# Three PSUM banks for the convolutions, transposes two heads behind, rank tables behind the sixth block

## The chip, the cores and the metric

The kernel runs on one core of a Trainium2 chip. The metric is the device time of one execution in microseconds (us); where several executions were timed, their median. The core's engines run beside each other and meet at semaphores: TensorE (PE: matmuls, with a separate row PEld for its weight loads), VectorE (DVE), ScalarE (ACT), GpSimd (POOL) and the queues that issue DMAs (SPq, ACTq, POOLq). The profile's times count from the first instruction of the profiled execution.

## The reference

`x` is 128 rows (batch) of 32 heads of 512 positions. A state-space layer turns each head into a causal convolution with a kernel computed from the parameters, and masks each row at its own length. The 4096 resulting tokens of 512 values go through a mixture of 16 experts (four per token) plus one shared expert, and the sum is added to `x`:

```python
K = _get_kernel(log_dt, C, log_A_real, A_imag, L)      # 32 heads x 512
y = irfft(rfft(u, 2 * L) * rfft(K, 2 * L))[..., :L] + u * D[:, None]
y = y * (arange(L) < length[:, None])                  # (128, 32, 512)
scores = sigmoid(y @ gate_w.T) + bias                  # 16 experts
topk_w, topk_idx = top_k(scores, 4)                    # normalised to weights cw
out = sum over e of (silu(y @ Wg[e].T) * (y @ Wu[e].T) * cw[e]) @ Wd[e].T
out = x + out + silu(y @ Sg.T) * (y @ Su.T) @ Sd.T
```

## The kernel before

The work has three stages. From 0 to about 125 us it builds the convolution kernels and convolves the 32 heads; from there to about 268 us it runs the shared expert over all tokens (eight units, `unit_step`) while it sorts the tokens by expert (`slots`); after that it runs the experts over sorted tiles of 128 tokens (`turn_of`). The change lies in the first stage.

**Heads and blocks.** Four heads make a block `tb` (eight blocks). The loop near the end of the first stage takes heads 0 and 1 alone and then pairs (2,3), (4,5) to (30,31). For a pair, `convolve` (L601) runs four matmuls a head on TensorE into a PSUM bank `py` (L607), and VectorE multiplies the bank by the length mask into `yb` (L625). I call this product "mask h". Behind each head `behind_head` (L951) issues other work: on given heads the next piece of the convolution kernels (`waves`, on VectorE and ScalarE, and `kernels`, on VectorE and GpSimd with small matmuls into `pk`, L407, read by `krow`, L415), the load of the next strip of kernels (`kernel_strip`, L433), a step of the rank tables (`ranks`), the gate's matmuls (`gates` L652, `sums` L669), routing (`route`, on VectorE, from L691) and the transposes of one head (`turn_y`: four transposes by `to_rank`, L631, and a ScalarE copy, L632). I call this "turn h".

**Order.** TensorE's order is the order of the program text: the loop stands in `tc.manual_schedule(engines={PE})`. For VectorE, ScalarE, GpSimd and the DMA queues a planner orders the instructions at compile time by its own estimate of when each can start. Each engine then runs its list strictly in order. Edges added by hand (`dep`, `behind_masks`, `later`) hold some VectorE instructions behind others.

**PSUM.** There are eight banks: `ps_m`, `ps_g`, `ps_u` and `ps_o` have two each. `py` takes the two of `ps_g`, head q of a block the bank q % 2. `turn_y` takes `ps_u`. `ps_m` carries `parts` of the gate, `cw_ps` of the weights and the small products of `ranks` (`by_rank_ps` L520, `k_u_ps` L540, `row_ps` L559). `ps_o` carries `pk` and the scores `pg`.

**Rank tables.** `ranks` is a generator of four steps, run behind heads 13 to 16. Step one casts `to_rank_h` (L517) and multiplies into `by_rank_ps` (L520); step two computes `reach` from it and multiplies into `k_u_ps` (L540); step three copies `k_u` and computes remainders (L239 to L554); step four multiplies into `row_ps` (L559) and writes `unit_rows` (L565). `k_u` is first read at head 31, the others later.

Of the kernel before, what the change touches and what calls it, by code (L numbers as in the profile page):

```python
# [28 lines left out]
F32 = mybir.dt.float32  # L29
# [6 lines left out]
PSUM = bass.MemoryType.PSUM  # L36
SYNC = mybir.DependencyInfo(mybir.DependencyClass.Sync, mybir.DependencyReason.DATA)

P = 128
B, H, L, N = 128, 32, 512, 64  # L40
E, TOPK, I = 16, 4, 256
KT = L // P
IT = I // P
HB = 4
NB = H // HB
RB = 2
# [28 lines left out]
LA, LB = 32, 16  # L75
# [4 lines left out]
def ssm_moe_kernel(  # L80
# [15 lines left out]
    nc = tc.nc  # L96
# [6 lines left out]
    ps_m = ctx.enter_context(tc.tile_pool(name="ps_m", bufs=2, space=PSUM))  # L103
    ps_g = ctx.enter_context(tc.tile_pool(name="ps_g", bufs=2, space=PSUM))
    ps_u = ctx.enter_context(tc.tile_pool(name="ps_u", bufs=2, space=PSUM))
    ps_o = ctx.enter_context(tc.tile_pool(name="ps_o", bufs=2, space=PSUM))


    conv = ctx.enter_context(ExitStack())
    ks1 = conv.enter_context(tc.tile_pool(name="ks1", bufs=1))  # L110
    yp = conv.enter_context(tc.tile_pool(name="yp", bufs=2))
    xp = conv.enter_context(tc.tile_pool(name="xp", bufs=2))


    def small(name, shape, src, dtype=F32):
# [42 lines left out]
    def dep(of, on, why):  # L158
        tc.add_manual_dep(of.ins, on.ins.name, SYNC, reason=why)
# [219 lines left out]
    def kernels(c0, n, mag, cos, sin):  # L379

        cs = slice(c0, c0 + n)
        other = nc.gpsimd if c0 else nc.vector

        for j in range(2):
            rows = slice(j * N, (j + 1) * N)
            nc.vector.tensor_mul(f_r[rows, cs, j, :], cos[rows, :, LA:], mag[rows, :, LA:])
            other.tensor_mul(f_i[rows, cs, j, :], sin[rows, :, LA:], mag[rows, :, LA:])

        shape = [P, n, LA]
        e_r, e_i, g_r, g_i, g_t = (  # L390
            wide(t, n * LA, most=NMAX * LA).rearrange("p (c a) -> p c a", a=LA)
            for t in ("ge_r", "ge_i", "gg_r", "gg_i", "gg_t")
        )
        nc.vector.tensor_mul(e_r, cos[:, :, :LA], mag[:, :, :LA])
        other.tensor_mul(e_i, sin[:, :, :LA], mag[:, :, :LA])
        by_r = ct_r[:, cs].unsqueeze(2).to_broadcast(shape)
        by_i = ct_i[:, cs].unsqueeze(2).to_broadcast(shape)
        nc.vector.tensor_mul(g_r, e_r, by_r)
        other.tensor_mul(g_t, e_i, by_i)
        nc.vector.tensor_add(g_r, g_r, g_t)  # L400
        nc.vector.tensor_mul(g_i, e_r, by_i)
        other.tensor_mul(e_i, e_i, by_r)
        nc.vector.tensor_sub(g_i, g_i, e_i)
        pk = ps_o.tile([P, n, 2 * LB], F32, tag="o", name=f"pk{c0}")
        for c in range(n):
            for g, f in ((g_r, f_r), (g_i, f_i)):
                nc.tensor.matmul(  # L407
                    pk[:LA, c, :],
                    lhsT=g[:, c, :],
                    rhs=f[:, c0 + c, :, :].rearrange("p j b -> p (j b)"),  # L410
                    start=(f is f_r),
                    stop=(f is f_i),
                )
        krow = ks1.tile([LA, 2 * NMAX, LB], F32, tag="krow", name=f"krow{c0}")[:, : 2 * n, :]
        last = nc.vector.tensor_add(  # L415
            krow,
            pk[:LA, :, :].rearrange("a c (j b) -> a (c j) b", j=2),
            dsk[:, 2 * c0 : 2 * (c0 + n), :],
        )
        kd = d1.tile([2 * n, L + PAD], F32, tag=f"kd{c0}", name=f"kd{c0}")  # L420
        nc.sync.dma_start(out=kd[:, L:], in_=zero[: 2 * n, :])
        nc.sync.dma_start(out=kd[:, :L].rearrange("h (a b) -> a h b", a=LA), in_=krow)
        for h in range(2 * c0, 2 * (c0 + n)):
            kd_of[h] = kd[h - 2 * c0 : h - 2 * c0 + 1, :]
        return last
# [11 lines left out]
        strip[tb] = s  # L437


    def keep_warm(on, n):  # L440
        warm = ps_u.tile([P, KT, P], F32, tag="u", name="warm")
        for _ in range(n):
            mm = nc.tensor.matmul(
                warm,
                lhsT=ones,
                rhs=ones.unsqueeze(1).to_broadcast([P, KT, P]),
                start=True,
                stop=True,
            )
            dep(mm, on, "in TensorE's order")  # L450
        return mm
# [5 lines left out]
    chunk_last = {0: chunk0}  # L457
# [51 lines left out]
    def ranks():  # L509

        to_rank_h = const.tile([P, P], F16, tag="to_rank_h", name="to_rank_h")
        last_chunk = chunk_last[max(chunk_last)]

        def later(op):
            dep(op, last_chunk, "later in VectorE's order")

        later(nc.vector.tensor_copy(to_rank_h, to_rank))  # L517

# [76 lines left out]
            by_number(m, lo, mid, some)  # L595


    pys = [ps_g.tile([P, L], F32, tag="g", name=f"py{i}") for i in range(2)]
    skip = {}

    def convolve(tb, qs, xt, yb):  # L601
        def products(n):
            c0 = n * TS
            for q in qs:
                for jt in range(KT):

                    nc.tensor.matmul(  # L607
                        pys[q % 2][:, c0 : L - jt * P],
                        lhsT=xt[:, jt, q, :],
                        rhs=strip[tb][:, q, jt * P + c0 :],  # L610
                        start=(jt == 0),
                        stop=(jt == KT - 1 or L - (jt + 1) * P <= c0),
                    )
                    if L - (jt + 1) * P <= c0:
                        break

        if len(qs) == 1:
            products(0)
        else:

            if not skip:
                skip[0] = nc.tensor.value_load(skips[0:1, 0:1], min_val=0, max_val=SKIPS - 1)
            by_number(skip[0], 0, SKIPS - 1, products)
        for q in qs:
            masks.append(nc.vector.tensor_mul(yb[:, q, :L], pys[q % 2], within))  # L625

    def turn_y(h, yb):
        q = h % HB
        pt = ps_u.tile([P, KT, P], F32, tag="u", name=f"pt{h}")
        for kt in range(KT):  # L630
            nc.tensor.transpose(pt[:, kt, :], yb[:, q, kt * P : (kt + 1) * P], to_rank)  # L631
        return nc.scalar.copy(  # L632
            yT[:, :, :, h, :].rearrange("p u k b -> p k u b"),
            pt.rearrange("p k (u b) -> p k u b", u=NU),
        )
# [7 lines left out]
    def gates(tb):  # L643


        if tb % RB == 0:

            pool, tag = (ps_o, "o") if tb + RB < NB else (ps_m, "m")
            pgs[tb // RB] = pool.tile([P, 512], F32, tag=tag, name=f"pg{tb}")
        parts = ps_m.tile([P, NU, HB, UB], F32, tag="m", name=f"parts{tb}")  # L650
        for kt in range(KT):
            mm = nc.tensor.matmul(  # L652
                parts[kt * QC : (kt + 1) * QC],
                lhsT=gw[:, kt, :],
                rhs=yT[:, :, kt, tb * HB : (tb + 1) * HB, :],
                start=True,
                stop=True,
            )
            parts_last[:] = [mm]
        pool, bufs = (yp, 2) if tb + 1 < NB else (sp, 1)  # L660
        by_head[tb] = pool.tile(
            [P, HB, NU, UB], F32, tag="by_head", name=f"by_head{tb}", bufs=bufs
        )
        nc.scalar.copy(by_head[tb].rearrange("p h u b -> p u h b"), parts)
# [286 lines left out]
    def behind_head(h):  # L951

        tb, q = divmod(h, HB)
        if h in waves_at:
            made_waves[waves_at[h]] = waves(*waves_at[h], 0)[0]
        if h in kernels_at:
            c = kernels_at[h]
            chunk_last[c[0]] = kernels(*c, *made_waves[c])
            behind_masks(chunk_last[c[0]])

        if strips[-1] in (tb, tb + 1) and strips[-1] < NB and strips[-1] * HB in kd_of:
            kernel_strip(strips[-1])
            strips.append(strips[-1] + 1)
        if 13 <= h <= 16:
            next(rest_of_ranks, None)
        if h in weights_at:
            weights_out(weights_at[h])
        if q == 2 and tb > 0:
            gates(tb - 1)
        last = h == H - 1  # L970
        if h > 0:
            turn_y(h - 1, ybs[(h - 1) // HB])
        if q == 3 and tb > 0 and not last:
            sums_and_route(tb - 1)
        if last:

            sums_and_route(tb - 1)
            k_us[0] = nc.tensor.value_load(of_ranks["k_u"][0:1, 0:1], min_val=1, max_val=KT)
            turned = turn_y(h, ybs[tb])
            gates(tb)  # L980
            return turned

    def sums_and_route(tb):
        sums(tb)
# [19 lines left out]
        dep(x_out, turned, "behind the convolutions")  # L1004
    by_rank, reach, k_u, unit_rows = (of_ranks[k] for k in ("by_rank", "reach", "k_u", "unit_rows"))
    conv.close()
    cst = ctx.enter_context(tc.tile_pool(name="cst", bufs=1))
    gp = ctx.enter_context(tc.tile_pool(name="gp", bufs=2))
    fp = ctx.enter_context(tc.tile_pool(name="fp", bufs=2))
# [343 lines left out]
```

## Time and profile before

| what | value |
|---|---|
| median of 3 runs (lowest, highest) | 916.95 us (914.7, 918.01) |
| the profiled execution: device time | 916.38 us |
| its span, first to last instruction | 914.7 us |
| TensorE busy in the span | 873.1 us, 95% |
| VectorE busy in the span | 415.0 us, 45% |
| mean granted TensorE clock | 0.994 |
| VectorE busy from 60 to 82 us | 20.54 of 22 us |
| TensorE busy from 60 to 82 us | 17.45 of 22 us |

The last two rows are from busy times by window; they show why a share over the whole span says little of this stage. TensorE counts as busy from a matmul's start to its modelled end, so a matmul at half clock is also "busy". An idle gap is printed behind the row that ended it, in the form `[2.13 <-DVE yb L625]`: 2.13 us of waiting, ended by VectorE's write of `yb` at line 625.

### The profile page before, as it was taken

The page shows a single profiled execution, that of the slowest core. Times are in us where ns is not written, and L with a number is a line of the kernel's source. Part 1 is how long each engine was busy: PE and PEld are TensorE (multiplying, and loading weights), DVE is VectorE, ACT ScalarE, POOL GpSimd, SP SyncE. Part 2 cuts the span into 40 slices and gives each one's busy share as a digit, 9 for nine tenths or more (in the row PEclk, how much of TensorE's full clock was granted, in tenths as well). Part 3 has the DMA queues.
Part 4 walks back from the last instruction along what each step waited for, and adds up shares of the span by engine and source line. Part 5 has one row for each costly group of instructions (what it writes and reads, how often), then busy time and mean ns, then how long its engine had stood idle before and what let it go on. Part 6 is the DMA issues. An engine that isn't in the chain of part 4 may idle for free.

```text
span 914.7 us, 14680 instructions
## 1 busy us (share of the span) xinstructions
PE 873.1 (95%) x2976; PEld 445.6 (49%) x2976; DVE 415.0 (45%) x1488; ACT 188.8 (21%) x379; POOL 420.3 (46%) x372
## 2 busy tenths in 40 slices
PE   2998999999999999999999999999999999999994
PEld 1666754444544444444444544444444544444441
DVE  8986674967812334423343334333433333344332
ACT  1122221211221122212221222112221112122221
POOL 2210010422474456645565456545645455566554
PEclk9999999999999999999999999999999999999998
DMA  5675866795698667866677667656756656667675
GB/s 201 206 271 175 276 228 212 184 225 121 126 215 214 131 111 128 148 156 114 118 134 175 111 110 139 118 106 109 141 108 108 113 96 116 108 130 134 107 126 100
DMA packets 54710, 136.03 MB, mean 149 GB/s; under 512 B 12432, under 2 KB 12592, under 8 KB 50992
## 3 DMA queue, kind: packets, MB, share of 16 engines
q0 software_dynamic: 36256, 89.77, 53.7%
q1 hardware_dynamic: 14096, 36.15, 11.6%
q10 hardware_dynamic: 4224, 8.39, 2.5%
q8 instruction: 76, 1.25, 0.5%
q14 instruction: 58, 0.48, 0.2%
HBM read 288.08 MB, written 60.64 MB: 381 GB/s over the span
## 4 chain that ended last, share of the span: by engine, by line
PE 67%; SPq 2%; issue 1%; POOL 0%; DVE 0%; ACT 0%; POOLq 0%; ACTq 0%
PE g L1189 34%; PE o L1215 24%; PE m L1157 4%; PE u L1207 3%; PE o L1076 1%; SPq L1240 1%; SPq L1294 0%; SPq L1276 0%; SPq L1275 0%; SPq L1277 0%; POOL out L1225 0%; SPq L1012 0%; DVE zt L1201 0%; ACT sgt L1200 0%; POOLq L1294 0%
## 5 line engine op out<-in xcount | busy, mean ns | idle before, releaser
L1189 PE MATMUL g<-store,yt 128*128 x742 | 343.2, 596 | 2.0 <-issue 1.4
L1225 POOL DMA_INDIRECT out<-ob,put x134 | 212.1, 1583 | 235.1 <-DVE junk L1164 190.1
L1215 PE MATMUL o<-store,zT 128*128 x536 | 252.0, 592 | 0.0
L1201 DVE SCALAR_TENSOR_TENSOR zt<-g,wt,sgt 128x256 f32<-128x256 f32 x135 | 65.3, 484 | 306.5 <-ACT sgt L1200 299.1
L1189 PEld LDWEIGHTS g<-store,yt 128*128 128x128 f32 x742 | 130.4, 190 | 118.8 <-issue 117.6
L1215 PEld LDWEIGHTS o<-store,zT 128*128 128x128 f32 x536 | 101.6, 190 | 128.6 <-issue 124.2
L1026 POOL DMA_INDIRECT yg<-y_rows,get x140 | 138.0, 986 | 49.7 <-issue 28.6
L1224 DVE COPY ob<-o 128x512 f32<-128x512 f32 x134 | 92.7, 692 | 109.2 <-PE o L1215 101.8
L1163 ACT COPY yt<-m 128x512 f32<-128x512 f32 x136 | 79.6, 585 | 225.9 <-PE m L1157 216.2
L1200 ACT ACTIVATE sgt<-g 128x256 f32<-128x256 f32 x135 | 51.8, 383 | 268.8 <-PE g L1189 226.3
L1085 POOL DMA_INDIRECT out<-ob,unit_rows x32 | 50.3, 1571 | 92.4 <-ACT ob L1083 57.7
L1157 PEld LDWEIGHTS m<-ident,yg 128*128 128x128 f32 x373 | 48.7, 141 | 72.2 <-issue 71.8
L607 PE MATMUL py<-strip,xt 128*128 128x192 f32 (+7 forms) x256 | 64.0, 404 | 0.2 <-DMA strip<-kd 0.2
L1157 PE MATMUL m<-ident,yg 128*128 128x128 f32 x373 | 63.0, 273 | 0.6 <-issue 0.5
L1076 PE MATMUL o<-store,z 128*128 128x512 f32 x128 | 57.6, 597 | 1.3 <-ACT yt L1163 1.3
L1210 DVE COPY zT<-u 128x256 f32<-128x256 f32 x134 | 56.4, 421 | 0.6 <-PE u L1207 0.6
L607 PEld LDWEIGHTS py<-strip,xt 128*128 128x128 f32 x256 | 44.4, 195 | 19.0 <-issue 13.4
L1207 PE MATMUL u<-ident,zt 128*128 128x128 f32 x268 | 51.2, 273 | 0.6 <-DVE zt L1201 0.6
L1061 PE MATMUL g<-store 128*128 128x512 f32 x92 | 42.9, 602 | 1.3 <-issue 0.9
L1061 PE MATMUL u<-store 128*128 128x512 f32 x92 | 42.2, 593 | 0.0
L910 DVE TENSOR_SCALAR cols<-tpos_h,stl,tok 128x143 f16<-128x143 f16 x128 | 41.9, 332 | 0.0
L1076 PEld LDWEIGHTS o<-store,z 128*128 128x128 f32 x128 | 23.5, 190 | 27.0 <-issue 25.3
(285 smaller groups left out, 493.7 us busy)
## 6 DMA issues: line engine op xcount, KB each, us to landing
store<-in_w_all SPq DMA_DIRECT2D x143, 1536.0 KB
xt<-in_x_t SPq DMA_DIRECT2D x8, 1024.0 KB
y_rows<-yb ACTq DMA_DIRECT2D x8, 1024.0 KB
out<-in_x POOLq DMA_DIRECT2D x8, 1024.0 KB
strip<-kd SPq DMA_DIRECT2D x7, 1024.0 KB
yg<-y_rows,get POOLq DMA_INDIRECT x140
out<-ob,put POOLq DMA_INDIRECT x134
strip<-kd SPq DMA_DIRECT2D x4, 256.0 KB
```

The costliest lines, as they stand in the source:

```text
L607: nc.tensor.matmul(pys[q % 2][:, c0 : L - jt * P], lhsT=xt[:, jt, q, :], rhs=strip[tb][:, q, jt * P + c0 :], start=(jt == 0), stop=(jt == ...
L1026: nc.gpsimd.indirect_dma_start(out=at(yg, t), out_offset=None, in_=y_rows[:, :], in_offset=bass.IndirectOffsetOnAxis(ap=made["get"][:, t : ...
L1061: nc.tensor.matmul(ps[it], lhsT=w_sh[:, c0 : c0 + P], rhs=yT[:, u, kt, :, :].rearrange("p h b -> p (h b)"), start=(kt == KT - n), stop=(kt ...
L1076: nc.tensor.matmul(po, lhsT=at(zu, u)[:, it, q * P : (q + 1) * P], rhs=w_sh[:, c0 : c0 + L], start=(it == 0), stop=(it == IT - 1),)
L1157: nc.tensor.transpose(pt[:, q, :], at(yg, t)[:, q * P : (q + 1) * P], ident)
L1163: nc.scalar.copy(at(yt, t), pt)
L1189: mm = nc.tensor.matmul(pgu, lhsT=at(yt, t)[:, q, :], rhs=ring_flat[:, bass.ds(w0s[t] + q * 2 * I, 2 * I)], start=(q == KT - n), stop=(q = ...
L1201: nc.vector.scalar_tensor_tensor(at(zs, t), pgu[:, I:], at(wts, t), sg, ALU.mult, ALU.mult)
L1207: nc.tensor.transpose(at(p_z, t)[:, it, :], at(zs, t)[:, it * P : (it + 1) * P], ident)
L1215: mm = nc.tensor.matmul(po, lhsT=at(zts, t)[:, it, :], rhs=ring_flat[:, bass.ds(w0s[t] + WD + it * L, L)], start=(it == 0), stop=(it == IT ...
L1224: nc.vector.tensor_copy(ob, po)
L1225: add = nc.gpsimd.indirect_dma_start(out=out, out_offset=bass.IndirectOffsetOnAxis(ap=made["put"][:, t : t + 1], axis=0), in_=ob, in_offse ...
```

## The change

It does four things.

1. A third bank `py2` stands beside the two of `ps_g`, and heads take the three in turn: head h uses bank h % 3.
2. While convolutions run, `ps_o` is not open. Its two banks form a pool `ps_c` with one bank for `py2` and one for `pg`; `pk` moves to `ps_m`. `ps_o` opens when the convolutions' pools close. The warm-up matmuls write `py2`.
3. Behind head h the transposes are those of head h - 2 instead of h - 1. Behind head 29 two heads' transposes are issued (27 and 28), so that the last two heads are as before.
4. The four steps of `ranks` come behind heads 24 to 27, and the instructions that were held behind the last piece of convolution kernels are now held behind the last mask issued, that of head 25 when step one begins.

```diff
-    ps_o = ctx.enter_context(tc.tile_pool(name="ps_o", bufs=2, space=PSUM))
...
+    ps_c = conv.enter_context(tc.tile_pool(name="ps_c", bufs=1, space=PSUM))
...
-        pk = ps_o.tile([P, n, 2 * LB], F32, tag="o", name=f"pk{c0}")
+        pk = ps_m.tile([P, n, 2 * LB], F32, tag="m", name=f"pk{c0}")
...
+    pys = [ps_g.tile([P, L], F32, tag="g", name=f"py{i}") for i in range(2)]
+    pys.append(ps_c.tile([P, L], F32, tag="y", name="py2"))
...
-        warm = ps_u.tile([P, KT, P], F32, tag="u", name="warm")
...
-                warm,
+                pys[2].rearrange("p (k b) -> p k b", k=KT),
...
-        last_chunk = chunk_last[max(chunk_last)]
+        last_mask = masks[-1]
 
         def later(op):
-            dep(op, last_chunk, "later in VectorE's order")
+            dep(op, last_mask, "later in VectorE's order")
...
-    pys = [ps_g.tile([P, L], F32, tag="g", name=f"py{i}") for i in range(2)]
...
+        heads = [(q, pys[(tb * HB + q) % len(pys)]) for q in qs]
...
-            for q in qs:
+            for q, py in heads:
...
-                        pys[q % 2][:, c0 : L - jt * P],
+                        py[:, c0 : L - jt * P],
...
-        for q in qs:
-            masks.append(nc.vector.tensor_mul(yb[:, q, :L], pys[q % 2], within))
+        for q, py in heads:
+            masks.append(nc.vector.tensor_mul(yb[:, q, :L], py, within))
...
-            pool, tag = (ps_o, "o") if tb + RB < NB else (ps_m, "m")
+            pool, tag = (ps_c, "o") if tb + RB < NB else (ps_m, "m")
...
-        if 13 <= h <= 16:
+        if 24 <= h <= 27:
             next(rest_of_ranks, None)
...
-        if h > 0:
-            turn_y(h - 1, ybs[(h - 1) // HB])
+        for each in turns_at(h):
+            turn_y(each, ybs[each // HB])
...
+    def turns_at(h):
+
+        if h < H - 3:
+            return [h - 2] if h > 1 else []
+        return [h - 2, h - 1] if h == H - 3 else [h - 1]
...
+    ps_o = ctx.enter_context(tc.tile_pool(name="ps_o", bufs=2, space=PSUM))
```

## The prediction

> **What bounds the kernel now.** I read the busy shares, the waits of TensorE (PE), and the timelines of PE and VectorE (DVE) over the first stage. The page first:
>
> ```profile
> PE 873.1 (95%) x2976; PEld 445.6 (49%) x2976; DVE 415.0 (45%) x1488; ACT 188.8 (21%) x379; POOL 420.3 (46%) x372
> PE 67%; SPq 2%; issue 1%; POOL 0%; DVE 0%; ACT 0%; POOLq 0%; ACTq 0%
> ```
>
> PE carries the program, and the chain that ended last is PE from 268 us on. From 125 us to the end the waits of PE add up to a few us, none of them on an instruction that the change touches. So what PE gains or loses in the first stage reaches the end in full. The waits of PE from 20 to 130 us:
>
> ```profile
> PE pt L631 <- DVE yb L625: 4.9, 3, 2.4
> PE pk L407 <- DVE gg_r L400: 0.9, 1, 0.9
> PE parts L652 <- ACT store L632: 0.7, 1, 0.7
> ```
>
> The reader is to see one thing: of some 7 us of idle PE, 4.9 is transposes that wait for masks. The timeline says where, here by rows of PE:
>
> ```profile
> 62.98 0.17 PE L520 MATMUL by_rank_ps<-num_len,to_rank_h 128*128 128x2 f16 x1
> 65.27 0.63 PE L631 MATMUL pt<-to_rank,yb 128*128 128x128 f32 x4 [2.13 <-DVE yb L625]
> 65.74 5.52 PE L607 MATMUL py<-strip,xt 128*128 128x448 f32 x16
> ...
> 74.46 3.87 PE L607 MATMUL py<-strip,xt 128*128 128x448 f32 x16
> 78.17 0.17 PE L559 MATMUL row_ps<-row_u,same_mod 128*128 128x8 f16 x1
> 78.19 0.63 PE L631 MATMUL pt<-to_rank,yb 128*128 128x128 f32 x4
> 81.25 0.63 PE L631 MATMUL pt<-to_rank,yb 128*128 128x128 f32 x4 [2.42 <-DVE yb L625]
> ```
>
> Counting pairs, these are turns 12 and 16. And the pair of 65.74 takes 5.52 us where others take 3.87: windows of 1 us show why (busy times, then PEclk):
>
> ```profile
> 67.00:68.00 1.00, 1.00 (x4) 0.80 (x3) 0.98 (x9) 0.00 (x0) 0.00 (x0) 0.50 0.06 25
> 68.00:69.00 1.00, 1.00 (x4) 0.87 (x4) 1.00 (x11) 0.00 (x0) 0.00 (x0) 0.50 0.00 0
> ```
>
> After the first wait PE ran at half clock for 3.4 us (0.83 in the window before these, 0.96 in the one from 70), a loss of 5.52 - 3.87 = 1.65. Last, DVE's own list:
>
> ```profile
> 64.45 0.68 DVE L625 TENSOR_TENSOR yb<-py,within 128x512 f32<-128x512 f32 x1
> ...
> 70.26 0.69 DVE L625 TENSOR_TENSOR yb<-py,within 128x512 f32<-128x512 f32 x1 [0.70 <-PE py L607]
> ...
> 80.28 0.23 DVE L403 TENSOR_TENSOR gg_i<-gg_i,ge_i 128x64 f32<-128x64 f32 x1 [0.19 <-POOL ge_i L402]
> 80.42 1.28 DVE L625 TENSOR_TENSOR yb<-py,within 128x512 f32<-128x512 f32 x2
> ```
>
> Mask 16 starts at 80.42, three us after its convolution, because routing and the last piece of the convolution kernels (to L403) stand ahead of it. From 59 to 81 us DVE is behind, and PE waits for it. After 82 us DVE is idle half of the time.
>
> **The change part by part.** I make the sum as PE's lost time from 23 to 125 us, before and after, in the profiled execution.
>
> Before: 0.91 (first `pk`), 0.16 and 0.32 (at 34 and 35 us), 2.13, 2.42, 0.20 (a strip, at 100 us), 0.67 and 0.33 (at the end), together 7.14, and 1.65 of half clock: 8.79.
>
> *Transposes two heads behind.* The waits of turns 12 and 16 go: these turns now come after the next pair. Early on, turn 2 is no longer in front of pair (4,5), but `pk` at 34 us still waits for L403. PE reaches it at 29.33 (turn 0 no longer ahead) + 3.62 for the pair + 0.56 for turn 0 = 33.51, and starts its halves at 33.95 and 34.36 with 0.16 between: 0.60 idle in place of 0.48. Pair (4,5) starts at 35.05, not 35.52: one turn is owed, 0.47 of lead. At head 29 it is paid back: turns 26, 27, 28 stand in a row, and turn 28 needs the bank that ScalarE empties of turn 26. From the rows at 115: a turn is 0.46, the copy starts 0.64 after the turns and takes 0.59. Turn 28 could start at 0.93 and starts at 1.30: 0.37 new.
>
> *Three banks: what is late next.* Head h+3 needs mask h. Pair (18,19) puts head 19 in the bank of head 16, so it waits for mask 16. When is that? I leave DVE's order as it is (its work is the same but for the rank tables). It starts its backlog 0.47 earlier, loses the 0.70 wait at 70.26 (PE is no longer slow), and about 0.4 of rank instructions (some 18 of 0.14 to 0.28, but most fit in the gaps of dependent chains: the rows at L543 and L552 to L561 give 0.1 and 0.3). So 80.42 - 0.47 - 0.70 - 0.4 = 78.85, plus 0.68 for the mask and 0.15 to PE (81.10 to 81.25 in the trace): 79.68. PE meanwhile: pair (12,13) from 58.34 for 3.72, turns 10 and 11 0.93, pair (14,15) 3.72 (bank of head 12: mask 12 ends at 64.66, head 15 starts at 64.9, just in time), the block to the next pair 3.27 (71.19 to 74.46), pair (16,17) 3.71, two turns 0.93, head 18 1.86: 76.48. **New wait: 79.68 - 76.48 = 3.2 us.** The whole gain over before at this point is only what pair (18,19) had left: it ends at 81.54, not 85.48, and one turn is still owed.
>
> *Half clock.* The row: idle for 2.13 us, half clock for 3.4 us thereafter; but idle for 2.42 us at 79 to 81, full clock. The Trainium skill, "TensorE: Matmul & The Clock Gate", Part 1, says that a free-running window of about 3.4 us is watched and that an idle one throttles; its summary asks for no gaps over about 3 us. By that rule a gap of 2.13 costs nothing, and before's half clock disagrees: about half a window idle sufficed. A window that ended at the drop (66.66) began at 63.25 and held 2.0 idle of 3.4; the next boundaries, 76.9 and 80.3, split the second gap so that no window held more than 1.5. A gap of 3.2 puts at least 1.75 into one window in about nine phases of ten. I take the row: 1.65 again (the rule alone, with a gap split over two windows: 0).
>
> *Rank tables behind heads 24 to 27.* This is the price that the diff doesn't name. The cast L517 is held behind mask 25, and the matmul L520 stands in PE's order right behind pair (24,25). Before, that cast was done at 52.6, ten us ahead. At pair (24,25) the trace has the pair's end at 104.03 and mask 25 at 104.23; DVE's next instruction starts 0.60 later, the cast takes 0.21, and 0.15 to PE: 105.19, **1.16 of idle PE**, with turns 22 and 23 and pair (26,27) queued behind. Then by_rank's copy (0.10), three comparisons, a sum and a cast (0.14 to 0.15 each, 0.18 apart where dependent, as at 148 us) until `k_u_ps`: ready 1.1 after by_rank_ps began, turn 22 covers 0.55: **0.55 more**. Before, pair (14,15) lay between these two steps. Step three has no matmul; `row_ps` follows gates and turn 24 (1.5 us after the pair), when k_u's copy behind mask 27 is through: 0. All four steps issue no DMA and pass no queue but PE's and DVE's. The 3 us of DVE work they take lies at 104 to 110, where DVE waits 2.8 us a pair.
>
> *`pk` in ps_m, `pg` in one bank.* `pk` now alternates with `parts`, `cw_ps` and the rank products. Each is read within 2 us, and the tile two places on comes 4 us later: 0, except `cw_ps` at head 27, now two places behind `parts`: that copy ends 1.77 after the pair, PE arrives at about 1.65: 0.25 with the signal. Below nothing is excluded, none of them waits now. `pg` of the next pair of blocks is written 12 us after L691 has read the last: 0. `ps_o` opens long before `down` needs it: 0. Without that cover each would cost a copy, 0.6. The strips and y_rows follow PE, so 0.20 stays.
>
> After: 0.91 + 0.60 + 3.2 + 0.20 + 1.16 + 0.55 + 0.25 + 0.37 + 0.67 + 0.33 = 8.24, and 1.65: 9.89. Against 8.79 that is +1.1: 916.38 + 1.1 = **917.5**. The profiled execution is 0.57 under the median of 916.95 and within its runs, so a median after may lie that much above.
>
> **The rivals.**
> *Same waits, no half clock* (chance 0.15): -0.55, 915.8. For it: the 2.42 gap. Against: 3.2 is nearly a whole window.
> *The planner sets mask 16 ahead* (0.19): with other PSUM waits it plans anew, and puts masks before L386 to L403. Then the 3.2 and the 1.65 go: -3.8, 912.6; with the rank handshake half hidden by luck, 911.7. Against: in its plan nothing of PE between masks 15 and 16 changes but two small matmuls.
> *The handshake grows* (0.14), slower: at heads 24 and 25 the planner sets the remainders (about eight of 0.14) and `reach`'s preparation ahead of by_rank's copy. 1.1 more idle makes 2.8 of idle within 4 us, and a second half clock: +1.1 + 1.1 + 1.65, 920.2. It decides where PE's idle there passes 1.75 in one window. For it: these instructions come free with the same mask 25. Unknown further waits in ps_m add to this side, up to 922.
> The forecast, masks late and one half clock, has 0.52.
>
> **How the numbers follow.** No change can be told within 0.5%, 4.6 us: 912.4 to 921.5. The forecast and the first rival lie inside. Of the second some two thirds, with the runs' scatter and gains I don't see, lie below 912.4 (0.19 in all); of the third and unknown waits 0.11 lie above. The range from 911.5 to 921.0 leaves out the ends of these two.
>
> **What would show it.** Right: no wait of `pt` (L631) on `yb`; a wait of about 3 us of `py` (L607) on DVE near 77 us, in the middle of a pair; a stretch at 0.5 clock behind it; waits at L520 of 1.2 and at L540 of 0.5 near 100 us. Wrong: mask 16 early (no wait at 77), the rank matmuls without a wait, a wait at L407 or L652, or the second stage beginning more than 3 us earlier or later than before's 125.3.

## The result and the profile after

The kernel after takes 913.41 us (median of 22 runs, 911.94 to 917.47) against 917.0 us before (22 runs): ratio 0.9961, 95% interval 0.9949 to 0.9974. That is a real gain, of about 0.4%, and inside the half per cent within which the prediction said that no change could be told. But 917.5 had been forecast, a small loss, and 913.41 came. The profiled execution of after took 913.5 us (span 911.8), that of before 916.38: 2.9 less. The second stage begins at 122.79 in place of 125.3, so nearly all of the gain is made in the first stage, as the prediction assumed.

After's page, the busy shares and the chain that ended last by engine:

```profile
PE 872.7 (96%) x2976; PEld 445.0 (49%) x2976; DVE 414.7 (45%) x1488; ACT 188.8 (21%) x379; POOL 420.1 (46%) x372
...
PE 92%; DVE 2%; SPq 2%; issue 2%; POOL 0%; ACT 0%; DMA 0%; ACTq 0%; DVEq 0%; POOLq 0%
```

PE still carries the end (the chain is followed back over nearly the whole span here, 92% of it PE, where before it was 67%). PE's work is the same to 0.5 us; what changed is where PE stands still. After's waits of PE from 20 to 130 us:

```profile
PE pk L407 <- DVE gg_r L400: 2.3, 2, 1.6
PE by_rank_ps L523 <- DVE to_rank_h L520: 1.1, 1, 1.1
PE parts L656 <- ACT store L636: 0.7, 1, 0.7
PE k_u_ps L543 <- DVE reach_b L541: 0.6, 1, 0.6
```

The waits of transposes for masks (4.9 us before) are gone. Nor is there the 3.2 us wait for a bank that the prediction put in their place: no row `py` on `yb`. The two rank matmuls now wait (I call these two waits the handshake, since TensorE and VectorE there wait for each other). After's timeline of PE (start, duration, instruction, idle time ahead of it), which answers to before's from 63 to 81 us and goes on to the rank matmuls:

```profile
62.40 3.79 PE L611 MATMUL py<-strip,xt 128*128 128x448 f32 x16
69.37 3.87 PE L611 MATMUL py<-strip,xt 128*128 128x448 f32 x16
73.95 3.79 PE L611 MATMUL py<-strip,xt 128*128 128x448 f32 x16
...
97.49 0.18 PE L523 MATMUL by_rank_ps<-num_len,to_rank_h 128*128 128x2 f16 x1 [1.12 <-DVE to_rank_h L520]
98.75 0.17 PE L543 MATMUL k_u_ps<-unit,reach_b 128*1 128x8 bf16 x1 [0.58 <-DVE reach_b L541]
99.34 5.47 PE L611 MATMUL py<-strip,xt 128*128 128x448 f32 x16
```

Pairs (14,15), (16,17) and (18,19) run at their usual 3.8 to 3.9 us with no wait ahead; pair (18,19) ends at 77.67, where before it ended at 85.48. Of these 7.8 us 2.5 are left when the second stage begins. One turn, about 0.5, was only put off; most of the rest is given back at 96 to 105 us: 1.12 and 0.58 of waiting, and pair (26,27) at 5.47. After's windows of 1 us (busy times by engine, then the granted clock) show why that pair is slow:

```profile
100.00:101.00 1.00, 1.00 (x3) 0.56 (x2) 0.00 (x0) 0.12 (x1) 0.00 (x0) 0.50 0.14 53
101.00:102.00 1.00, 1.00 (x3) 0.61 (x3) 0.00 (x0) 0.00 (x0) 0.00 (x0) 0.50 0.04 16
```

In this execution half clock falls here, where in before's it fell on pair (14,15). Last, VectorE's list in after, to set beside before's 70 to 81 us:

```profile
73.90 0.68 DVE L629 TENSOR_TENSOR yb<-py,within 128x512 f32<-128x512 f32 x1
...
74.67 0.68 DVE L629 TENSOR_TENSOR yb<-py,within 128x512 f32<-128x512 f32 x1
...
76.72 0.26 DVE L337 SCALAR_TENSOR_TENSOR wm<-wq,ws 128x96 f32<-128x96 f32 x1
...
79.16 0.22 DVE L403 TENSOR_TENSOR gg_i<-gg_i,ge_i 128x64 f32<-128x64 f32 x1
```

This is the finding to explain. Before, masks 16 and 17 stood behind L403, at 80.42. Now they stand at 73.90 and 74.67, ahead of L337. L403 itself moved by only 1.1 us. The masks changed places in VectorE's list, which nothing in the diff orders by hand.

In the prediction's own bookkeeping PE loses in after 1.56 and 0.72 (`pk`), 1.12, 0.58, 0.17 (`row_ps`), 0.24 (turn 28), 0.68 and 0.33: 5.4 idle, and 5.47 - 3.87 = 1.6 at half clock, together 7.0 in place of 8.79. The first pair also began 0.8 us earlier (22.56), which the longer first wait of `pk` takes back. 1.8 and 0.8 are 2.6; the stage is 2.5 shorter.

### The profile page after: what moved, and what is told of

Its sections match the earlier page's. It is cut to its first block, busy times and chain, and to the rows that moved or that the text cites. A ratio compares the mean times of both kernels' runs of the same rounds, so it can differ in the third digit from the quotient of the medians.

```text
span 911.8 us, 14680 instructions
## 1 busy us (share of the span) xinstructions
PE 872.7 (96%) x2976; PEld 445.0 (49%) x2976; DVE 414.7 (45%) x1488; ACT 188.8 (21%) x379; POOL 420.1 (46%) x372
## 4 chain that ended last, share of the span: by engine, by line
PE 92%; DVE 2%; SPq 2%; issue 2%; POOL 0%; ACT 0%; DMA 0%; ACTq 0%; DVEq 0%; POOLq 0%
PE g L1200 35%; PE o L1226 24%; PE o L1087 6%; PE py L611 6%; PE g L1072 5%; PE u L1072 4%; PE m L1168 4%; PE u L1218 3%; PE pt L635 1%; PE pa L902 1%; PE parts L656 1%; PE pg L673 1%; SPq L1251 1%; DVE wq L269 0%; PE py L446 0%
```

## The experiments

Three questions are open: which part of the change moved masks 16 and 17; whether the late masks would have cost what was forecast; and what the rank matmuls behind heads 24 and 25 cost. Ratios are to before (median 916.75 to 917.15 us in the three sets of runs), with their 95% intervals. Each expectation says what its theories are.

**The rank tables alone, on before.**

```diff
-        last_chunk = chunk_last[max(chunk_last)]
+        last_mask = masks[-1]
...
-            dep(op, last_chunk, "later in VectorE's order")
+            dep(op, last_mask, "later in VectorE's order")
...
-        if 13 <= h <= 16:
+        if 24 <= h <= 27:
```

> Only the rank tables move behind heads 24 to 27 (held behind mask 25); two banks and turn h - 1 as before. Theory A: it is the move of the rank tables that lets the planner set masks 16 and 17 ahead of the last piece of the convolution kernels in VectorE's list. Then the 2.4 us wait of turn 16 goes, the 2.1 us wait of turn 12 and the half clock behind it stay, and about 1.1 + 0.6 us at L520 and L540 are new: 917.0 - 2.4 + 1.7 = 916.3, or 917.9 with a second half clock. Theory B: the whole gain is the banks' and turns': the wait of turn 16 stays and the handshake is added, 918.7 to 920.3.

914.37 us, ratio 0.9965 (0.9950 to 0.9979): within the interval as much as the whole change. VectorE's timeline of this kernel:

```profile
75.00 0.68 DVE L625 TENSOR_TENSOR yb<-py,within 128x512 f32<-128x512 f32 x1
75.77 0.69 DVE L625 TENSOR_TENSOR yb<-py,within 128x512 f32<-128x512 f32 x1
77.24 0.26 DVE L337 SCALAR_TENSOR_TENSOR wm<-wq,ws 128x96 f32<-128x96 f32 x1
79.44 0.22 DVE L403 TENSOR_TENSOR gg_i<-gg_i,ge_i 128x64 f32<-128x64 f32 x1 [0.18 <-POOL ge_i L402]
```

Two banks, transposes one head behind, and yet masks 16 and 17 stand ahead of L337 and the wait of turn 16 is gone. Turn 12 still waits (1.53), and the rank matmuls wait 1.05 and 0.58. So the rank tables' leaving heads 13 to 16 is enough to move the masks.

**The banks and transposes alone: after, with the rank tables put back.**

```diff
-        last_mask = masks[-1]
+        last_chunk = chunk_last[max(chunk_last)]
...
-        if 24 <= h <= 27:
+        if 13 <= h <= 16:
```

> Three banks and transposes two heads behind, the rank tables behind heads 13 to 16 as before. Theory A: VectorE's list keeps masks 16 and 17 behind L403, as the prediction assumed. Head 19 then waits about 3 us for its bank near 77 us, with half clock behind it or not; no waits at the rank matmuls: 914.5 to 916.1. Theory B: with a bank more and two heads of slack nobody waits for masks any more: no such wait, 910.5 to 911.5.

916.35 us, ratio 0.9992 (0.9977 to 1.0006): nothing gained. The masks are late again (81.92 and 82.95, L403 at 78.03), but the expected bank wait isn't there, for PE comes late itself: pair (18,19) starts at 83.69, when mask 16 is done. This kernel's timeline of PE, and the row of VectorE that ends the wait:

```profile
62.06 3.79 PE L611 MATMUL py<-strip,xt 128*128 128x448 f32 x16
...
71.67 0.17 PE L543 MATMUL k_u_ps<-unit,reach_b 128*1 128x8 bf16 x1 [5.19 <-DVE reach_b L541]
...
71.47 0.14 DVE L541 CAST reach_b<-reach_sum 128x1 bf16<-128x1 f32 x1
```

And its windows behind that wait:

```profile
72.00:76.00 4.00, 4.00 (x20) 2.37 (x12) 3.96 (x29) 1.96 (x5) 0.00 (x0) 0.50 0.41 125
76.00:80.00 4.00, 4.00 (x12) 2.79 (x12) 1.71 (x8) 0.23 (x1) 1.45 (x5) 0.50 0.76 240
```

PE reaches the second rank matmul early and stands 5.19 us before it, and then runs at half clock for some ten us (0.50 in each window of 1 us from 71 to 81). The profiled execution took 919.35 us, 3.0 above the median, so half clock of that length need not be in every run. No theory had this wait. It is the one that before's trace hides. Before's timeline of PE, and VectorE's row there:

```profile
71.71 0.17 PE L540 MATMUL k_u_ps<-unit,reach_b 128*1 128x8 bf16 x1
...
71.39 0.15 DVE L538 CAST reach_b<-reach_sum 128x1 bf16<-128x1 f32 x1
```

There `k_u_ps` ran without any wait, because PE was late by its own stalls. Its input `reach_b` comes from a chain of small instructions that VectorE does between other work, and is ready at 71.5 to 71.6 in both kernels.

**The rank steps from the second on, one block later.** The rank tables early again, but steps two to four behind heads 18 to 20; first on after's banks and transposes:

```diff
-        last_mask = masks[-1]
+        last_chunk = chunk_last[max(chunk_last)]
...
-        if 24 <= h <= 27:
+        if h in (13, 18, 19, 20):
```

> Three banks and turns two heads behind, with the rank steps behind heads 13, 18, 19 and 20 in place of 13 to 16: only the second rank matmul and what follows it move, by one block. Theory A: the one instruction that spoilt the kernel with three banks alone is the second rank matmul behind head 14, for which TensorE waited 5.2 us. Then this kernel has no wait over 1 us from 60 to 110 us, masks 16 and 17 early in VectorE's list, and no handshake near 97 us: about 910 to 911, like the eased kernel. Theory B: it is VectorE's extra work in its busy stretch that costs, not the place of the matmul: 915 to 916.

910.69 us, ratio 0.9931 (0.9913 to 0.9950). Masks 16 and 17 are early (74.04, 74.81), no rank matmul waits, and the second stage begins at 118.91. This kernel's waits of PE from 20 to 130 us, the longest ones:

```profile
PE pk L407 <- DVE gg_r L400: 1.4, 2, 0.7
PE parts L656 <- ACT store L636: 0.7, 1, 0.7
PE py L611 <- DMA strip<-kd: 0.7, 1, 0.7
```

Then on before, where it is one line (`13 <= h <= 16` becomes `h in (13, 18, 19, 20)`):

> The kernel before, with two banks and turns one head behind, and only the rank steps two to four moved, from behind heads 14 to 16 to behind 18 to 20. Theory A: the place of the second rank matmul alone makes the planner set masks 16 and 17 late; moving it by one block is worth the wait of turn 16 and leaves that of turn 12: about 912.5, as with the eased rank steps on two banks. Theory B: on two banks it needs the move of all VectorE's rank work: 915 or more.

913.0 us, ratio 0.9961 (0.9946 to 0.9975): the whole change's ratio, by moving three steps of the rank tables by a few heads. VectorE's timeline of this kernel:

```profile
71.09 0.15 DVE L538 CAST reach_b<-reach_sum 128x1 bf16<-128x1 f32 x1
...
77.00 0.69 DVE L625 TENSOR_TENSOR yb<-py,within 128x512 f32<-128x512 f32 x1 [0.65 <-PE py L607]
...
78.03 0.69 DVE L625 TENSOR_TENSOR yb<-py,within 128x512 f32<-128x512 f32 x1 [0.17 <-PE py L607]
...
80.02 0.26 DVE L337 SCALAR_TENSOR_TENSOR wm<-wq,ws 128x96 f32<-128x96 f32 x1
```

Masks 16 and 17 stand ahead of L337. Turn 12 still waits, 2.27, with half clock behind it (pair (14,15) takes 5.04).

The first rank step is in its old place in both. So it is the place of the later steps that decided where masks 16 and 17 stood. Three steps moved together, but two rivals to the second matmul fall away. VectorE's rank work did not leave the busy stretch: `reach_b` is made at 71.09 here and at 71.39 in before, the remainders and `row_u` (L554) still come ahead of L337, and only the copy of `k_u` (0.15 us) goes behind L403. And `row_ps`, the other matmul that moved, stood behind pair (16,17) in PE's order, where it could not hold up the convolutions of these masks. What the planner reckoned is in no record; that it held PE in its plan at `k_u_ps` and put these masks behind L403 for that reason is inferred from its orders in these kernels, and the 5.19 us show that such a hold was there to be reckoned with.

**The late masks, in after's order otherwise.** After, with masks 16 and 17 held by an edge behind the last L403, as the prediction had assumed:

```diff
+        pieces[c0] = nc.vector.tensor_sub(g_i, g_i, e_i)
...
+            if h == 20:
+                for late in masks[16:18]:
+                    dep(late, pieces[c[0]], "later in VectorE's order")
```

> The changed kernel with an edge that holds masks 16 and 17 behind L403 of the last piece of convolution kernels in VectorE's list, where the prediction left them. Nothing else changes. Theory A: the prediction's sum failed only in VectorE's order. Then head 19 waits for its bank in the middle of pair (18,19) for about 2.5 us (L403 ends near 77.6, mask and signal 0.9 later, head 18 ends near 75.9), the handshake near 97 us stays: 913.7 + 2.5 = 916.2, or 917.8 with half clock behind it. Theory B: three banks and two heads of slack absorb late masks: 913.7, and the prediction's bank wait was wrong as well.

918.51 us, ratio 1.0010 (0.9993 to 1.0027): the gain of the whole change is gone. VectorE's timeline, then PE's, and then the windows:

```profile
78.36 0.23 DVE L403 TENSOR_TENSOR gg_i<-gg_i,ge_i 128x64 f32<-128x64 f32 x1 [0.19 <-POOL ge_i L402]
78.68 1.29 DVE L629 TENSOR_TENSOR yb<-py,within 128x512 f32<-128x512 f32 x2
```

```profile
74.25 1.95 PE L611 MATMUL py<-strip,xt 128*128 128x448 f32 x8
79.43 3.38 PE L611 MATMUL py<-strip,xt 128*128 128x448 f32 x8 [3.23 <-DVE yb L629]
```

```profile
80.00:83.00 3.00, 3.00 (x12) 2.01 (x14) 0.84 (x2) 0.00 (x0) 0.00 (x0) 0.50 0.44 162
```

A bank wait of 3.23 us in the middle of pair (18,19), ended by mask 16, and half clock behind it (head 19 takes 3.38, head 18 1.95). The second stage begins at 126.48, 1.2 later than before's; by its runs the kernel can't be told from before. This is the kernel that was forecast: 3.2, half clock, +1.1.

**The rank matmuls at heads 24 and 25 taken off PE's path.** After, with the later steps one head or two further on and held behind a mask two earlier:

```diff
-        last_mask = masks[-1]
+        last_mask = masks[-3]
...
-        if 24 <= h <= 27:
+        if h in (24, 26, 27, 28):
```

> The changed kernel with the rank steps behind heads 24, 26, 27 and 28 and held behind mask 23, so that the cast is done before pair (24,25) ends and a pair of convolutions lies between the first two rank matmuls. Theory A: the waits of 1.12 and 0.58 us go and with them the half clock (1.6): 913.4 - 3.3 = 910.1. Theory B: the half clock near 100 us has another cause than this idle time: only 1.7 goes, 911.7. Theory C: the time is taken up again by a strip that comes late: 913.

910.46 us, ratio 0.9922 (0.9899 to 0.9945). Neither matmul waits, pair (26,27) takes 3.79, the second stage begins at 119.46, 3.3 earlier than after's, about the two waits and the half clock, 1.70 and 1.6. With the kernel of the second rank step above this beats both before and after.

The same eased rank tables on before, without the banks and transposes:

> Two banks and turns one head behind as before; only the rank steps move, behind heads 24, 26, 27 and 28 and held behind mask 23. It tells what the banks and turns are worth once the rank tables are out of the way. Theory A: the wait of turn 12 (1.5 us in the kernel with the rank tables alone moved) stays, and the handshake of 1.6 goes: 914.4 - 1.6 = 912.8, against 910.5 with three banks. Theory B: banks and turns are worth nothing: 910.5.

912.16 us, ratio 0.9951 (0.9936 to 0.9965). Turn 12 waits 1.43, and the second stage begins at 120.76. Against the kernel just above, three banks and later transposes are worth 1.3 us in the trace; the two ratios' intervals overlap, so by the runs this is not clear of noise.

**Halves of the other part.** After with the transposes one head behind, as before:

```diff
-        if h < H - 3:
-            return [h - 2] if h > 1 else []
-        return [h - 2, h - 1] if h == H - 3 else [h - 1]
+        return [h - 1] if h > 0 else []
```

> The changed kernel with three banks but turn h - 1 behind head h as before. Theory A: the wait of turn 12 for its mask comes back (about 1.5 us near 63 us), since TensorE's own list puts it there whatever bank is free: about 914.4, as with the rank tables alone moved. Theory B: the third bank is what removes the waits: no wait of pt on yb, 913.4 or less.

915.72 us, ratio 0.9981 (0.9968 to 0.9994). The wait of turn 12 is back (1.15), `by_rank_ps` waits 1.66 and `k_u_ps` 0.53, and strips 1.4 in four places. And after with two banks:

```diff
-        heads = [(q, pys[(tb * HB + q) % len(pys)]) for q in qs]
+        heads = [(q, pys[q % 2]) for q in qs]
```

> The changed kernel with turns two heads behind but two banks (head q on bank q % 2). Theory A: pair (14,15) now waits at its first head for mask 12, about 1.2 us near 64 us: 914.5. Theory B: turns two heads behind alone remove the waits: no wait of py on yb, 913.5.

916.78 us, ratio 0.9993 (0.9975 to 1.0010). PE waits 1.86 ahead of pair (12,13) and 1.58 ahead of pair (20,21), both put down to VectorE's work (L386, L271) that these pairs don't read; the expected wait near 64 us isn't there, since PE comes late. What makes these two waits isn't settled. A strip of kernels that comes late is a candidate for the second: its load was issued at 77.62 here, at 72.70 in after. It is shown only that this kernel, with later transposes and no third bank, gains nothing, and that a third bank without them leaves turn 12 waiting.

**Is the half clock part of the handshake?** After, run once more:

> The changed kernel once more, beside the three runs of this call. Its handshake leaves TensorE idle for 1.1 and 0.6 us near 97 us in every execution, since VectorE's list is fixed. Theory A: whether half clock follows is a matter of where the window falls, so this profile may show the pair (26,27) at 3.8 us in place of 5.5. Theory B: it follows each time: 5.5 again. Time 913.4 by either.

913.99 us, ratio 0.9968 (0.9954 to 0.9982). The same two waits, 1.12 and 0.59, but this kernel's windows are:

```profile
100.00:101.00 1.00, 1.00 (x5) 0.66 (x4) 0.00 (x0) 0.38 (x1) 0.00 (x0) 1.00 0.07 27
101.00:102.00 1.00, 1.00 (x7) 0.81 (x6) 0.00 (x0) 0.00 (x0) 0.00 (x0) 1.00 0.00 0
```

Full clock, and pair (26,27) takes 3.79. Six traces have these two waits without filler (1.04 to 1.66, and 0.53 to 0.59); pair (26,27) is slow in two of them (5.47 in after, 5.39 with two banks). So the half clock comes in some executions and not in others of the same kernel. Then after with idle PE filled: five matmuls of ones into an idle bank ahead of `by_rank_ps`, two ahead of `k_u_ps`.

```diff
+        if h in (24, 25):
+            fill({24: 5, 25: 2}[h])
```

> The changed kernel with 5 matmuls (ones by ones, into the idle bank) ahead of the first rank matmul and 2 ahead of the second, which fill PE's idle time there with work that nobody reads. Theory A: idle PE brings the half clock, so the clock stays at 1.00 near 100 us and the pair (26,27) takes 3.8 in place of 5.5: 913.4 - 1.6 = 911.8. Theory B: the clock falls whatever PE does there: 913.4 or a little more, with 0.50 near 101 us.

913.48 us, ratio 0.9954 (0.9937 to 0.9972), where 911.8 was expected. The profiled execution shows full clock behind the filler and 3.79 for pair (26,27), but so does after's second trace without filler. From the end of pair (24,25) to pair (26,27) 2.97 us pass, as in after: the filler held nothing up. The time can't be told from after's. Whether filler keeps the clock up here is left open.

## Why the prediction was wrong, point by point

*PE is the bound and the first stage is passed on in full*: right. 2.5 us less there, 2.9 in the profiled execution.

*Transposes two heads behind*: right in kind. The waits of turns 12 and 16 are gone (that of turn 16 goes by the masks' new place alone, as the rank tables on before showed). The first `pk`, left at 0.91, took 1.56, which the first pair's earlier start makes up. `pk` at 34 us was put at 0.60 and took 0.72, turn 28 at 0.37 and took 0.24.

*"I leave DVE's order as it is"*: this step failed, and with it the sign. The order is the planner's, and it changed. The sum built on it was right to 0.1 us: with the masks held where I left them, the bank wait is 3.23 (3.2 forecast), the half clock comes, and the second stage begins 1.2 later (1.1 forecast). What made the order different is named in the rival that I set at 0.19, in the sentence against it: "nothing of PE between masks 15 and 16 changes but two small matmuls". One of these, `k_u_ps`, is the cause as far as the runs separate it. I weighed it by its duration, 0.17 us. What counted was how long its input lets TensorE's fixed list stand, 5.19 us where nothing else delays PE. Before's trace has no wait at that row, and I took that for no cost. The rival itself came out at 912.6, against 913.5 for the profiled execution: it lacked the 1.6 of half clock that fell there. That 913.41 lies inside the stated range is the range's width; the forecast inside it had the wrong sign.

*The handshake behind heads 24 and 25*: right. 1.16 and 0.55 forecast, 1.12 and 0.58 measured. `cw_ps` was put at 0.25; 0.17 is seen instead at `row_ps`.

*Half clock*: the row was the better guide than the rule. I had named 1.75 us idle in one window as the point of decision, an estimate from where I supposed the windows to lie; two waits of together 1.70 (1.62 with two banks) were enough in two traces of six. In after's profiled execution the half clock fell at the handshake, which the slower rival had only for a longer handshake. It is chance, about 1.6 us of it, and belongs in the range, not in the forecast.

The gain is then: the rank steps from the second on out of PE's way (ratio 0.9961 by themselves, on two banks), and the banks and transposes (1.3 us in the trace, not clear of noise in the runs, once the rank tables are out of the way; nothing while they are not); less the handshake, which the eased version avoids.

## What to carry to other kernels

Where one engine's order is written by hand and another's is planned, a small instruction in the fixed list whose input comes late can reorder the other engine's list: here masks 16 and 17 moved by some six us. Ask of every moved instruction when its input comes, not only how long it takes; a trace in which its engine comes late shows no wait there. And move such a step to where its input has long been ready: that one line was worth as much here as the whole change.

## What the runs showed of the hardware

The granted clock fell to half after a wait of 2.13 us in before (1.65 lost), of 2.27 and of 3.23 in two experiments (pair (14,15) at 5.04, head 19 at 3.38), and after 1.12 and 0.58 with 0.7 between them in after; of six traces with such a pair of waits two had it. The 2.42 us of before and single waits of 1.15 to 1.86 were followed by none. A wait of 5.19 us was followed by some ten us at half clock, three times the 3.4 of before. The same kernel (after) had it in one trace and not in the next, so one trace cannot say what a gap near 2 us costs.
